# Where the absolute sums of the feed-forward weights are taken: VectorE's reduction, or ScalarE's absolute value with a second result

## The chip, the core and the metric

One core of one Trainium2 chip runs the whole kernel. Its engines have a queue of instructions each and run them in order: TensorE (PE, with its weight loads shown apart as PEld), VectorE (DVE), ScalarE (ACT), GpSimd (POOL), and SyncE (SP), which here issues nearly all transfers. The metric is the device time of one execution in microseconds; what is shown as the time before is the median of three runs. The profile is of one further execution: its span goes from the first to the last instruction, its time is taken around it.

## What is computed

A cross-attention layer and a feed-forward layer with quantized weights, on four batches of 512 tokens by 512 features, float32. Cut to what matters here:

```python
x = x + attention(layernorm(x), ctx, pos, Wq, Wkv, Wout, bout)     # 32 heads of 16, rotary positions
x = x + ffn(layernorm(x), w_fc, w_proj)                            # 512 -> 2048 -> 512

def ternarize_weights(w):
    gamma = jnp.mean(jnp.abs(w))                                   # one number for a whole matrix
    return jnp.sign(jnp.round(w / (gamma + EPS))) * gamma

def bitlinear(x, w):
    xn = layer_norm(x)
    x_hat = absmax_quant(xn)                                       # 128 levels a side
    return jnp.einsum('bsd,od->bso', x_hat, ternarize_weights(w))

def ffn(x, w_fc, w_proj):
    return bitlinear(jax.nn.gelu(bitlinear(x, w_fc), approximate=False), w_proj)
```

Both weight matrices have 2048 x 512 elements. Before their signs can be formed, the sum of all absolute values of the matrix has to be known. That sum is what the change is about.

## The kernel before

**Two parts.** The attention runs first, up to about 565 us; the feed-forward follows. The weights are summed and turned into signs during the attention, between its other work, and the signs go back to DRAM (wfc_d, wproj_d), from where the feed-forward loads them.

**Attention.** There are 32 groups (4 batches, 8 groups of 4 heads), and a group has 8 units. A unit of kind "l" makes scores (lp, L524) of which only the row maxima are wanted: VectorE takes them in one reduction of 128x1024 (mx, L538). A unit of kind "s" makes the scores again, transposed (sp, L563), adds the negated maxima by another matmul (L571, from mrows), and ScalarE takes the exponential (es, L575). Two s units together feed the weighted sum of values (av, L585), eight matmuls. lp runs some 12 units ahead of sp. lp and sp share three PSUM tiles (tag "s"), used in turn, so a new score tile needs the one three before it drained: an lp by VectorE, an sp by ScalarE.

**Order.** The order on all five queues is written out by hand. The units are strung together, s and l in turn, and cut into bursts of three. In burst k the kernel first runs what was put off to its start (run(k): copies out of PSUM by ScalarE, such as L430, L497, L381, L554 and L602), then the burst's units, then what was put off to its end (run(k, 1)), then the weighted sums that are due, then a "chore": projections, transposes, and the like (L344, L374, L550), which have one PSUM tile of their own. put_off(k, f, 1) puts f at the end of burst k.

**The weights.** The two matrices are cut into 32 pieces of 128x512 (chunk). At units 2 and 6 of every group from the first on, sum_chunk loads one piece into a buffer of tag "wch" (four buffers) and puts its sum off to the end of the fourth burst after. Each sum is one column of wsums. At groups 8 and 16 mean_abs adds 16 columns (L694) and sums over the partitions by a matmul. From group 9 on, at the same units and behind sum_chunk, sign_chunk loads a piece again into a "wch" buffer; two bursts later POOL compares it (low, L686), three bursts after that VectorE forms the signs (ws, L684), and one burst later SP stores them (L688).

So in groups 0 to 15 each group has two sums; from group 9 to 24 it has two pieces of signs. SP issues the loads of both (L667, L680), the stores of rotated queries and keys (L424), the loads of the stacks (L510), and the transfers of the attention's result (L603, L614, L615, L619, L623), all in one order; a load into a "wch" buffer waits at the head of SP's queue until that buffer is free.

**ScalarE's tables.** Sin, Exp and Gelu are each announced by one small activation ahead of their use (L817, L1015) or come with the first use (L247); the copies, casts and squares between them are on ScalarE too.

Of the kernel before, what the change touches and what calls it, by code (L numbers as in the profile page):

```python
# [11 lines left out]
AF = mybir.ActivationFunctionType  # L12
ALU = mybir.AluOpType
AX = mybir.AxisListType
# [17 lines left out]
def xattn_ffn(  # L32
# [13 lines left out]
    nc = tc.nc  # L46
# [248 lines left out]
    def put_off(k, f, end=0):  # L295
        later[end].setdefault(k, []).append(f)
# [70 lines left out]
    def tokens(b, t, ready=0):  # L367


        def step(tp, _):  # L370
            if t == 0:
                xT[b] = big.tile([P, KD, S], F32, name=f"xT{b}", tag="w4")
            for k in range(KD):
                nc.tensor.transpose(  # L374
                    tp[:, k * P : (k + 1) * P], xh[b, t][:, k * P : (k + 1) * P], ident
                )

        def post(tp, k):
            put_off(
                k + 1,  # L380
                lambda: nc.scalar.copy(  # L381
                    xT[b][:, :, t * P : (t + 1) * P], tp.rearrange("p (k n) -> p k n", k=KD)
                ),
            )
            if b > 0 and t + XH < NT:
                put_off(k + 1, lambda: normed(b, t + XH), 1)

        return Chore(f"xtp{b}_{t}", 1, step, post, 0.7, ready)
# [95 lines left out]
    def values(b, t):  # L484
        def step(p, k):
            product(
                p,
                ctx_tiles[b][:, k, t * P : (t + 1) * P],
                wkv_sb[:, k, D : 2 * D],
                k == 0,  # L490
                k == KC - 1,
            )

        def post(p, k):
            put_off(
                k + 1,
                lambda: nc.scalar.copy(  # L497
                    va[b % 2][:, t, 0 : NH * VS].rearrange("p (h d) -> p h d", d=VS)[:, :, 0:HD],
                    p.rearrange("p (h d) -> p h d", d=HD),
                ),  # L500
            )

        return Chore(f"vp{b}_{t}", KC, step, post)
# [43 lines left out]
    def place_maxima(i):  # L547
        def step(tp, _):
            for t in range(NT):
                nc.tensor.transpose(tp[:, t * P : (t + 1) * P], mparts[i % 2][:, t, :], ident)  # L550

        def post(tp, k):
            mrows[i] = apool.tile([P, S], F32R, name=f"mrows{i}", tag="mrows")
            put_off(k + 1, lambda: nc.scalar.copy(mrows[i], tp))  # L554

        return Chore(f"mtp{i}", 1, step, post, 0.7)
# [96 lines left out]
    wsums = const.tile([P, 2 * NW], F32, name="wsums")  # L653
# [3 lines left out]
    def chunk(c):  # L657
        if c < NW:
            k, n = divmod(c, FB)
            rows, cols = slice(k * P, (k + 1) * P), slice(n * 512, (n + 1) * 512)  # L660
            return wfcT[rows, cols], wfc_d[rows, cols], gam_fc
        rows = slice((c - NW) * P, (c - NW + 1) * P)
        return wprojT[rows, :], wproj_d[rows, :], gam_pr

    def sum_chunk(c, k):
        w = apool.tile([P, D], F32, name=f"wm{c}", tag="wch", bufs=4)
        nc.sync.dma_start(w, chunk(c)[0])  # L667
        put_off(
            k + 4,
            lambda: nc.vector.tensor_reduce(  # L670
                wsums[:, c : c + 1], w, AX.X, ALU.add, apply_absolute_value=True
            ),
            1,
        )

# [111 lines left out]
    c = heads(0, 0, "k")  # L787
# [4 lines left out]
    for t in range(NT):  # L792
        c = tokens(0, t)
# [5 lines left out]
    c = heads(0, 0, "q")  # L799
# [5 lines left out]
    for what in "kq":  # L805
        c = heads(0, 1, what)
# [14 lines left out]
    c = values(0, 0)  # L821
# [8 lines left out]
    for n in range(FIRST + 1):  # L830
# [11 lines left out]
        if n == NU + 1:  # L842
            c = place_maxima(0)
# [65 lines left out]
    for k, burst in enumerate(bursts):  # L909
        run(k)  # L910
        for kind, s in burst:
# [21 lines left out]
            if u in (2, 6):  # L933
                c = 2 * i + u // 4
                if c < 2 * NW:
                    sum_chunk(c, k)
                c -= 18
                if 0 <= c < 2 * NW:
                    sign_chunk(c, k)
# [21 lines left out]
        while due and due[0][0] <= k:  # L961
            _, j, c, e = due.pop(0)
# [17 lines left out]
        while True:  # L980
            if open_chore is None:
# [5 lines left out]
                elif queue and queue[0].ready <= k and not used_bank and credit >= queue[0].cost:  # L987
                    c = queue[0]
# [286 lines left out]
```

## Time and profile before

| | |
|---|---|
| time before, median of 3 runs | 841.18 us (840.21 to 842.34) |
| time of the profiled execution | 843.25 us |
| its span | 840.9 us |
| mean granted TensorE clock | 0.995 |
| POOL busy | 297.6 us (35%) |
| the sums, L670: VectorE, 128x512 float32 | 32 of 672 ns mean, 21.5 us |
| loads of the pieces for the sums, L667 | 32 of 256 KB, issued 48.6 to 314.7 us |
| forming the signs, L684: VectorE | 32, from 214.4 to 478.4 us |

How to read what follows. A row of a group of instructions gives line, engine, operation, what is written and read by the program's names, shapes and count; then busy time in us and the mean of one in ns; then the idle time of the engine just before them and what ended most of it. A row of the timeline gives start and length in us; rows that follow each other on an engine are merged (x2), and brackets give the idle time before and its releaser. A row of waits gives the total, how many times, and the longest. A row of a stretch gives its bounds and length, then busy time (and instructions) of PE, PEld, DVE, ACT and POOL, the granted TensorE clock, the share of the DMA engines and GB/s. A matmul's row overlaps the next one's, since they are pipelined; the distance from start to start says more than the length.

### The profile page before, as it was taken

Reading aid. Unit: us, or ns where it says so; the run is one execution under the profiler, and the core shown is the slowest. Engines: PE = TensorE matmul, PEld = TensorE weight load, DVE = VectorE, ACT = ScalarE, POOL = GpSimd, SP = SyncE. Lnnn points to the kernel's source line nnn. Section 1 sums busy time; section 2 is a strip of 40 time slices with the busy share of each in tenths; the row PEclk is TensorE's granted clock in tenths of the full one; section 3 lists DMA queues with packets and bytes.
Section 4 is the critical chain, followed back from the end, with each engine's and each line's share of the span. In section 5 each row is a group of like instructions: output and inputs, shape, how many; then the busy total and the mean of one; then the engine's idle time right before and its main releaser. Section 6 shows DMA issues by size and latency. Waiting matters only on the chain.

```text
span 840.9 us, 14326 instructions
## 1 busy us (share of the span) xinstructions
PE 816.2 (97%) x5572; PEld 435.0 (52%) x5572; DVE 613.9 (73%) x858; ACT 456.9 (54%) x604; POOL 297.6 (35%) x299
## 2 busy tenths in 40 slices
PE   8999999999999999999999999999999999999996
PEld 5234433444333334333333334337678888888885
DVE  7799778797878888787777867825465864964755
ACT  3256666575665546656555655576234544554442
POOL 2546274555823637576425621301000100100000
PEclk9999999999999999999999999999999999999999
DMA  7768595687585578949446657532000100100101
GB/s 247 215 209 300 188 329 186 204 292 258 197 296 164 171 265 258 314 168 301 159 151 215 225 179 277 182 110 88 1 0 1 51 1 0 51 1 1 51 0 51
DMA packets 75923, 133.65 MB, mean 159 GB/s; under 512 B 12240, under 2 KB 13776, under 8 KB 75344
## 3 DMA queue, kind: packets, MB, share of 16 engines
q1 hardware_dynamic: 74928, 132.08, 46.4%
q8 instruction: 44, 0.72, 0.3%
q10 hardware_dynamic: 928, 0.66, 0.3%
q14 instruction: 23, 0.19, 0.1%
HBM read 77.73 MB, written 53.94 MB: 157 GB/s over the span
## 4 chain that ended last, share of the span: by engine, by line
PE 81%; DVE 12%; issue 3%; POOL 1%; DMA 1%; ACT 1%; ACTq 0%; DVEq 0%; POOLq 0%; SPq 0%
PE hp L1048 14%; PE fp L1086 14%; PE av L585 12%; PE sp L563 8%; PE lp L524 7%; DVE mx L538 6%; PE sp L571 5%; PE qpq L344 5%; PE op L344 4%; PE vp L344 3%; PE kpk L344 3%; PE op L1167 2%; PE mtp L550 1%; PE xtp L374 1%; PE tot L1106 1%
## 5 line engine op out<-in xcount | busy, mean ns | idle before, releaser
L538 DVE TENSOR_REDUCE mx<-lp 128x2 f32<-128x1024 f32 x256 | 305.1, 1215 | 88.2 <-PE lp L524 87.9
L575 ACT ACTIVATE es<-sp 128x1024 f32<-128x1024 f32 x256 | 254.6, 1024 | 148.9 <-PE sp L571 140.7
L585 PE MATMUL av<-es,va 128*32 128x512 f32 x1024 | 136.9, 608 | 0.0
L563 PE MATMUL sp<-q_st,k_st 64*128 64x512 f32 x512 | 115.0, 445 | 7.3 <-DVE mx L538 6.2
L524 PE MATMUL lp<-k_st,q_st 64*128 64x512 f32 x512 | 111.8, 434 | 3.8 <-DMA q_st<-sl_q 1.9
L1056 ACT ACTIVATE h<-hp,gam_fc 128x512 f32<-128x512 f32 x64 | 44.1, 689 | 125.6 <-PE hp L1048 125.6
L1086 PE MATMUL fp<-wproj,hh 128*128 128x512 f32 x256 | 102.2, 399 | 0.0
L571 PE MATMUL sp<-mrows,sel 64*128 64x512 f32 x512 | 101.7, 393 | 0.2 <-ACT mrows L554 0.2
L1048 PE MATMUL hp<-dTh,wfc 128*128 128x512 f32 x256 | 100.0, 391 | 1.2 <-ACT dTh L758 1.2
L1048 PE MATMUL hp<-dTl,wfc 128*128 128x512 f32 x256 | 99.8, 390 | 0.2 <-DVE dTl L759 0.2
L1086 PE MATMUL fp<-wproj,hl 128*128 128x512 f32 x256 | 99.7, 390 | 0.0
L1075 DVE TENSOR_TENSOR acc<-acc,h 128x512 f32<-128x512 f32 x56 | 38.6, 690 | 71.4 <-ACT h L1056 71.4
L563 PEld LDWEIGHTS sp<-q_st,k_st 64*128 64x128 f32 x512 | 48.0, 184 | 81.9 <-DVE mx L538 42.3
L524 PEld LDWEIGHTS lp<-k_st,q_st 64*128 64x128 f32 x512 | 48.2, 185 | 75.1 <-ACT es L575 38.7
L624 POOL TENSOR_TENSOR aT<-aT,rb 128x512 f32<-128x512 f32 x16 | 22.0, 1374 | 129.7 <-DMA rb<-rden_d 108.3
L344 PE MATMUL qpq<-xT,wq_sb 128*32 128x512 f32 x512 | 63.5, 599 | 0.7 <-ACT xT L381 0.7
L1048 PEld LDWEIGHTS hp<-dTh,wfc 128*128 128x128 f32 x256 | 48.1, 188 | 12.0 <-ACT dTh L758 2.1
L1086 PEld LDWEIGHTS fp<-wproj,hh 128*128 128x128 f32 x256 | 48.1, 188 | 10.4 <-issue 0.7
L1048 PEld LDWEIGHTS hp<-dTl,wfc 128*128 128x128 f32 x256 | 48.1, 188 | 10.4 <-DVE dTl L759 0.5
L1086 PEld LDWEIGHTS fp<-wproj,hl 128*128 128x128 f32 x256 | 48.1, 188 | 10.3 <-issue 0.7
L571 PEld LDWEIGHTS sp<-mrows,sel 64*128 64x128 f32 x512 | 48.3, 185 | 5.9 <-ACT mrows L554 0.8
L224 POOL TENSOR_SCALAR r_a<-mv 128x1 f32<-128x1 f32 x16 | 4.7, 294 | 127.8 <-DVE mv L734 127.8
(149 smaller groups left out, 1054.9 us busy)
## 6 DMA issues: line engine op xcount, KB each, us to landing
k_st<-k_d SPq DMA_DIRECT2D x31, 512.0 KB
q_st<-q_d SPq DMA_DIRECT2D x31, 512.0 KB
av_d<-avs SPq DMA_DIRECT2D x32, 256.0 KB
k_d<-sh_k SPq DMA_DIRECT2D x30, 256.0 KB
k_d<-sl_k SPq DMA_DIRECT2D x30, 256.0 KB
q_d<-sh_q SPq DMA_DIRECT2D x30, 256.0 KB
q_d<-sl_q SPq DMA_DIRECT2D x30, 256.0 KB
wm<-in_wfcT SPq DMA_DIRECT2D x16, 256.0 KB
```

The lines of the kernel that those rows point to most:

```text
L344: nc.tensor.matmul(p[j * HP : (j + 1) * HP, :], w[:, j * HP : (j + 1) * HP], x, start=start, stop=stop,)
L524: nc.tensor.matmul(lp[:, h, :], q_st[i][rows, r, t * P : (t + 1) * P], k_st[i][rows, r, :], start=True, stop=True,)
L538: nc.vector.tensor_reduce(mx[i][:, t, :, r], lp, AX.X, ALU.max, negate=True)
L563: nc.tensor.matmul(sp[:, h, :], k_st[i][rows, r, c * P : (c + 1) * P], q_st[i][rows, r, :], start=True, stop=False,)
L571: nc.tensor.matmul(sp[:, h, :], sel[rows, r, :], mrows[i][rows, :], start=False, stop=True)
L575: nc.scalar.activation(es, sp, AF.Exp, scale=1.0 / math.sqrt(HD))
L585: nc.tensor.matmul(av[j * HP : (j + 1) * HP, :], va[b % 2][:, c, v0 : v0 + HP], es[r][:, h, :], start=c == 0, stop=c == NT - 1,)
L624: nc.gpsimd.tensor_tensor(aT[b][:, n, :], aT[b][:, n, :], rb, ALU.mult)
L1048: nc.tensor.matmul(hp, wfc_sb[k][:, f * P : (f + 1) * P], dT[b][half][:, k, :], start=half == 0 and k == 0, stop=half == 1 and k == KD - 1,)
L1056: nc.scalar.activation(hid[b, f], hp, AF.Gelu, scale=gam_fc[:, 0:1])
L1075: nc.vector.tensor_tensor(acc[b][0], old, x, ALU.add)
L1086: nc.tensor.matmul(outs[b][t], parts[b, f][half][:, t * P : (t + 1) * P], wproj_sb[f], start=half == 0 and f == 0, stop=half == 1 and f == ...
```

## The change

The sum of a piece moves from VectorE to ScalarE. There it is an activation with the function Abs, which writes the absolute values back over the piece and gives, as a second result (accum_out), their sum along the row. It is put off to the same burst, and stands at the end of that burst in ScalarE's order instead of VectorE's. The loads, the buffers, mean_abs and sign_chunk stay as they are; sign_chunk loads its piece again, so nothing reads the values written over.

```diff
@@ -667,9 +667,7 @@
         nc.sync.dma_start(w, chunk(c)[0])
         put_off(
             k + 4,
-            lambda: nc.vector.tensor_reduce(
-                wsums[:, c : c + 1], w, AX.X, ALU.add, apply_absolute_value=True
-            ),
+            lambda: nc.scalar.activation(w, w, AF.Abs, accum_out=wsums[:, c : c + 1]),
             1,
         )
```

## The prediction

> **What bounds the kernel now.** I read the page's busy times first, then the chain, then the costliest groups, the waits of TensorE's weight loads while the sums run, and last the timeline at each of the 32 sums.
>
> ```profile
> PE 816.2 (97%) x5572; PEld 435.0 (52%) x5572; DVE 613.9 (73%) x858; ACT 456.9 (54%) x604; POOL 297.6 (35%) x299
> ...
> PE 81%; DVE 12%; issue 3%; POOL 1%; DMA 1%; ACT 1%; ACTq 0%; DVEq 0%; POOLq 0%; SPq 0%
> ...
> L538 DVE TENSOR_REDUCE mx<-lp 128x2 f32<-128x1024 f32 x256 | 305.1, 1215 | 88.2 <-PE lp L524 87.9
> L575 ACT ACTIVATE es<-sp 128x1024 f32<-128x1024 f32 x256 | 254.6, 1024 | 148.9 <-PE sp L571 140.7
> ```
>
> TensorE holds 81% of the chain, VectorE 12%. So VectorE matters only where TensorE waits for a maximum (L538): the three tiles of tag "s" are shared by scores for the maxima (lp) and for the exponentials (sp), and each new tile waits until the one three before it is drained, by VectorE (lp) or ScalarE (sp).
>
> ```profile
> L670 DVE TENSOR_REDUCE wsums<-wm x32: 622/676/680, 63.5 to 323.6; 128x1 f32<-128x512 f32 x32
> ...
> 60.00:330.00 270.00, 266.26 (x2068) 106.28 (x2060) 225.50 (x285) 163.36 (x194) 146.62 (x123) 0.99 0.70 236
> ...
> PEld sp L563 <- DVE mx L538: 20.9, 37, 1.9
> PEld lp L524 <- ACT es L575: 19.8, 36, 0.8
> ```
>
> The sums run from 63.5 to 323.6 us. In 60 to 330 VectorE is busy 225.5 of 270 us (84%), ScalarE 163.4 (61%), so the move goes from the fuller engine to the emptier. But the weight loads' waits of some 20 us for either engine overstate it: most lie under a matmul that still runs. I therefore took TensorE's starts in the timeline. After a pair of matmuls into one tile the next pair usually starts 0.23 to 0.33 us later; only what is beyond is a stall. In front of sp (L563) that excess sums to about 9.7 us over 60 to 330, and most of it is not behind a sum.
>
> **What is removed.** 32 reductions of 0.672 us (21.5 us of VectorE); the next instruction behind one starts 0.55 to 0.60 us after it. At 16 of the 32 VectorE then sits idle 0.08 to 1.36 us until TensorE delivers the next lp: nothing gained there. Behind the others I looked whether the maximum that comes next is one TensorE stalls for, and took the lesser of the stall and the time that the maximum can move. The largest:
>
> ```profile
> 271.65 0.66 PE L550 MATMUL mtp<-ident,mparts 128*128 128x128 f32 x4
> ...
> 272.18 0.63 DVE L670 TENSOR_REDUCE wsums<-wm 128x1 f32<-128x512 f32 x1
> ...
> 272.72 2.34 DVE L538 TENSOR_REDUCE mx<-lp 128x2 f32<-128x1024 f32 x2
> ...
> 273.98 0.50 PE L563 MATMUL sp<-q_st,k_st 64*128 64x512 f32 x2 [1.67 <-DVE mx L538]
> ```
>
> The maxima start 0.54 us after the sum does, so 0.54 of the 1.74 us go; the rest is there because five other VectorE instructions came before. In the same way: 0.42 at 75 us (stalls of 0.09 and 0.33, maxima 0.60 earlier), 0.24 at 105.9, 0.55 at 173.6 to 174.8 (stalls 0.52 and 0.33, maxima 0.55 earlier), 0.19 at 205.6, 0.33 at 302.2, 0.54 at 310.1 to 311.2 (0.22 for the addition L646, 0.32 for sp). Sum: 0.42+0.24+0.55+0.19+0.54+0.33+0.54 = 2.8 us.
>
> **The clock.** The stall at 273.98 has a second price:
>
> ```profile
> 265.24:268.65 3.41, 2.88 (x30) 1.16 (x26) 3.41 (x5) 1.94 (x2) 1.53 (x2) 1.00 0.76 202
> ...
> 272.07:275.48 3.41, 1.57 (x13) 0.78 (x11) 3.41 (x5) 1.25 (x2) 0.00 (x0) 1.00 0.40 132
> 275.48:278.90 3.42, 3.42 (x20) 0.59 (x16) 2.75 (x6) 1.39 (x2) 0.00 (x0) 0.50 0.27 85
> ```
>
> TensorE was busy 1.57 of 3.41 us, and the next 3.41 us were granted half the clock: 1.7 us of work lost. With 0.54 us less stall that stretch would be busy 2.11 of 3.41 us, 62%, between this 46% and the 84% (2.88) that brought no dip. I count the dip as gone in the profiled execution. The three timed runs lie between 840.21 and 842.34 us, a spread wider than the dip, so some may not have had it; against their median I count half, 0.85 us.
>
> [...]
>
> **What is added.** Each sum becomes an ACTIVATE (Abs, written back over w) plus whatever delivers the second result. No row shows either. Nearest for the pass: Square, 128x512 float32 from SBUF to SBUF. For the delivery: nothing below, another full pass above; nearest is the smallest ACTIVATE, one column.
>
> ```profile
> L1073 ACT ACTIVATE sq<-h 128x512 f32<-128x512 f32 x60 | 37.7, 628 | 0.0
> ...
> L817 ACT ACT_TABLE_LOAD x1 | 1.3, 1283 | 0.0
> ...
> L817 ACT ACTIVATE exp<-ones 128x1 f32<-128x1 f32 x1 | 0.2, 203 | 0.0
> ```
>
> So A, the time for one sum, is 0.63 to 1.26 us; I take 0.63+0.20 = 0.83 (26.6 us in all). The Abs is queued in run(k, 1), behind the last exponential of burst k. Behind it wait the copies of burst k+1 (L602, L430, L381, L497, L554) and the next exponentials, and for those TensorE's tile three later and the weighted sums (L585). I listed for all 32 places the ScalarE idle time that follows (0 to 2.6 us), passed the remaining delay on, and set it against the time from the end of each delayed instruction to the start of the matmul that needs it. Copies have 0.6 us or more, av 1.8 us or more, and exponentials 0.38 or more, but for two places, this one and its twin at 181:
>
> ```profile
> 78.99 0.59 ACT L602 COPY avs<-av 128x512 f32<-128x512 f32 x1 [0.17 <-PE av L585]
> 79.55 0.59 ACT L381 COPY xT<-xtp 128x512 f32<-128x512 f32 x1
> 80.28 1.94 ACT L575 ACTIVATE es<-sp 128x1024 f32<-128x1024 f32 x2
> ...
> 81.38 0.50 PE L524 MATMUL lp<-k_st,q_st 64*128 64x512 f32 x2
> ```
>
> The first exponential ends at 81.31 and lp starts 0.08 us later, 0.055 being the least anywhere. The Abs stands before 78.99; of its 0.83 us the gaps 0.17 and 0.14 take 0.31, 0.52 reach the exponential, 0.49 TensorE. Twice that is 1.0 us of loss. The same working gives 0.6 us at A = 0.63, 1.6 at 1.0, 3.1 at 1.2, 3.7 at 1.26, 5.3 at 1.43: one more place at a time loses its slack.
>
> **What moves with it.** No DMA is added. The SP queue waits for these sums to free a "wch" buffer:
>
> ```profile
> SPq L680 <- DVE wsums L670: 35.9, 12, 7.4
> ```
>
> That is from SP's own waits (total, times, longest). Queued behind it are stores and loads of the next stacks. Comparing the ends at sums 17 to 31: the Abs would end 0.3 to 0.8 us later at six of them, up to 3.6 us earlier (272.80 against 269.3) at the rest; no stall of TensorE in that stretch ends with a DMA, so I count nothing. The total over the sums (L694, 188.62) now waits for ScalarE: the last Abs of that layer ends near 187.6, 1 us ahead; without that cover the signs start later, which feed only DRAM.
>
> **Sum.** In the profiled execution (span 840.9, time 843.25, the highest of the four times shown): -2.8 + 1.0 - 1.7 = -3.5, a span of 837.4. Against the median: 841.18 - 2.8 + 1.0 - 0.85 = 838.5 us. Below 0.3% (2.5 us) a measurement of this kernel can't tell a change from none.
>
> **Rivals.**
> 1. The gain goes into other VectorE work. L331 took 1.52 us at 170 beside a POOL instruction, against 0.54 elsewhere; casts L542 1.18 against 0.17. If the later three gains (0.54, 0.33, 0.54) are spent in such collisions and the dip stays, 1.4 - 1.0 remain: 840.8. For it: five other instructions in front of 273.98. Against: where maxima follow the sum directly, nothing is between.
> 2. The wait changes sides: exponentials held behind the Abs. It needs a dear second result, at L602, L381, L430 and the exponentials of sums 2, 7, 12, 14, 16, 18 and 20. It beats the 2.8 us from A = 1.16 and is slower by 2.5 from A = 1.43: 841.2 - 2.8 + 5.3 = 843.7. For it: no row shows the read. Against: one-column work costs 0.20.
> 3. Abs needs a table load of its own and Exp another after it: two of 1.283 for each sum, A = 3.2, loss 50.5: 889. Against: three loads in all, though Copy, casts and Square run between Exp and Gelu. [...]
> 4. The pass itself takes ScalarE a multiple of VectorE's time. [...] Against: 0.628 for Square on the same shape and type. [...]
> 5. All 9.7 us of stalls before sp go, and the dip: 841.2 - 9.7 - 1.7 + 1.0 = 830.8. Against: only 2.8 stand behind sums.
>
> **How the numbers follow.** Forecast 58%, its own range 836 to 840.5; 46 of it faster by over 2.5 us, 12 within. Rival 1 14% (within). Rival 2 18% (16 slower, 2 within). Rival 3 3%. Rival 4 1%. Rival 5 6%. So faster 0.52, same 0.28, slower 0.20. The range goes from 834.5, part of the way to rival 5, to 843.7, rival 2.
>
> **What would show it.** L670 as ACTIVATE near 0.63 us and a short second row on ACT; three table loads; VectorE's busy time down 21.5 us, ScalarE's up 20 to 27; the stalls at 75, 173 and 274 gone or near 1.2; new ones of half a microsecond where xT is copied (81 and 181); clock 1.00 near 275. Wrong if the ACT rows for a sum exceed 1.2 us, or TensorE waits for es at more than those two places.

## The result, and the profile after

| | before | after |
|---|---|---|
| median on the same chip, 20 runs each | 841.68 us (839.76 to 845.64) | 839.46 us (836.41 to 841.86) |
| profiled execution: time, span | 843.25, 840.9 us | 839.09, 837.3 us |
| mean granted clock of the profiled execution | 0.995 | 0.999 |

The ratio of the times is 0.9971, with an interval of 0.9959 to 0.9983: some 2.4 us faster (1.4 to 3.5). The predicted time was 838.5 us, the predicted span of the profiled execution 837.4.

Lines of the changed kernel's page: the span, busy time by engine, shares of the chain, and the two groups that drain the score tiles.

```profile
span 837.3 us, 14374 instructions
...
PE 812.9 (97%) x5572; PEld 434.6 (52%) x5572; DVE 597.8 (71%) x826; ACT 474.1 (57%) x668; POOL 297.2 (35%) x299
...
PE 81%; DVE 12%; DMA 2%; issue 2%; ACT 1%; POOL 1%; ACTq 0%; SPq 0%; DVEq 0%; POOLq 0%
...
L538 DVE TENSOR_REDUCE mx<-lp 128x2 f32<-128x1024 f32 x256 | 305.2, 1216 | 100.0 <-PE lp L524 99.7
L575 ACT ACTIVATE es<-sp 128x1024 f32<-128x1024 f32 x256 | 254.9, 1025 | 139.3 <-PE sp L571 130.7
```

The shape of the chain is what it was. VectorE has 32 instructions and 16 us less, ScalarE 64 instructions and 17 us more; the forecast had 21.5 less and 20 to 27 more. The rows of the sums are that long (21.5, and 20.1 + 6.4), but rows that overlap count once in the busy time, and on VectorE forming the signs of the first matrix rose from 14.6 to 17.5 us. VectorE's idle time ahead of the maxima rose from 88.2 to 100.0 us, so most of the time it won went into waiting for TensorE.

Groups of instructions on ScalarE in the changed kernel: the new line and the table loads.

```profile
L670 ACT ACTIVATE wm<-wm 128x512 f32<-128x512 f32 x32 | 20.1, 628 | 0.0
L670 ACT ACTIVATION_READ_ACCUMULATOR wm<-wm 128x1 f32 x32 | 6.4, 199 | 0.0
...
L247 ACT ACT_TABLE_LOAD x1 | 1.3, 1283 | 3.9 <-issue 3.9
L815 ACT ACT_TABLE_LOAD x1 | 1.3, 1283 | 0.0
L1013 ACT ACT_TABLE_LOAD x1 | 1.3, 1283 | 0.0
```

Each sum is two instructions: the pass, 0.628 us, as long as Square was, and a read of the accumulated sum, 0.199 us. There are three table loads, as before.

Three stretches of the changed kernel, with busy time by engine, granted clock, and DMA: first 60 to 330 us, then two beats of 3.41 us around the stall that stood at 274 us (now at 271). In the trace of the kernel before, half clock begins at 29.72, at 275.48 and, behind TensorE's last work, at 838.68 us; the first two stretches last 3.41 us each, and the second and third begin 72 and 237 such beats behind the first. I divided each trace into beats of this length, counted from a half clock of its own. From the start of the span they lie elsewhere from one execution to another (the first half clock begins at 29.72 us there, at 29.25 in the sixth run, at 28.8 in the tenth); those of this one are counted back from 835.45 us, where half clock begins behind TensorE's last work.

```profile
60.00:330.00 270.00, 265.60 (x2072) 106.75 (x2070) 212.78 (x257) 182.25 (x261) 149.33 (x126) 1.00 0.72 241
268.84:272.25 3.41, 2.17 (x20) 1.01 (x12) 3.38 (x6) 1.39 (x3) 0.00 (x0) 1.00 0.36 126
272.25:275.66 3.41, 3.22 (x24) 1.09 (x26) 3.38 (x7) 1.65 (x2) 0.25 (x1) 1.00 0.63 202
```

VectorE went from 225.5 to 212.8 us in the first, ScalarE from 163.4 to 182.3. TensorE is busy 2.17 of the 3.41 us of the beat with the stall (1.57 before), and no half clock follows.

The timeline of the changed kernel at that stall, TensorE and VectorE:

```profile
269.28 0.66 PE L550 MATMUL mtp<-ident,mparts 128*128 128x128 f32 x4
...
269.57 0.32 DVE L618 RECIPROCAL den<-den 128x32 f32<-128x32 f32 x1
269.80 2.29 DVE L538 TENSOR_REDUCE mx<-lp 128x2 f32<-128x1024 f32 x2
...
271.02 0.50 PE L563 MATMUL sp<-q_st,k_st 64*128 64x512 f32 x2 [1.08 <-DVE mx L538]
```

From the last transposition group to sp it is 1.74 us, where 0.59 is usual: a stall of 1.15. Before, the same distance was 2.33, a stall of 1.74. The sum that stood between the reciprocal and the maxima is gone, and so are 0.59 us.

SP's own wait for a "wch" buffer in the changed kernel (total, times, longest); the numbers of lines behind the change are two less:

```profile
SPq L678 <- ACT wm L670: 32.5, 9, 5.7
```

Before it was 35.9 us in 12 waits, the longest 7.4. No stall of TensorE hangs on it in either kernel.

**Where the 3.6 us between the two profiled spans lie.** I compared the start of the first sp of each of the 32 groups in the two traces. The changed kernel is 1.78 us ahead at group 0 already, before any sum is formed: the other execution had half a clock at 29.7 us, this one had none. It wins 1.85 us between groups 13 and 14 (0.59 of stall and about 1.25 of half clock). At the other steps 2.7 us are won and 2.7 lost, and from group 19 on the lead stays at 3.6. So apart from the two half clocks this pair differs by 0.6 us, and the first of the two cannot come from the change.

The steps with sums 1, 5, 13 and 28 and 29 are won about as forecast: 0.54, 0.25, 0.59 and 0.63 us, where the prediction had 0.42, 0.24, 0.55 and 0.87. The largest loss is 1.24 us from group 16 to 17. POOL and VectorE there, first in the changed kernel:

```profile
318.88 1.28 POOL L416 TENSOR_TENSOR oth_k<-oth_k,trig 128x512 f32<-128x512 f32 x1
320.11 1.30 POOL L417 TENSOR_TENSOR rot_k<-rot_k,trig 128x512 f32<-128x512 f32 x1
...
318.89 1.31 DVE L542 CAST mparts<-mx 128x16 fp32r<-128x16 f32 x1
320.23 1.21 DVE L543 TENSOR_TENSOR mparts<-mx,mparts 128x16 fp32r<-128x16 f32 x1
```

and the same two VectorE instructions before:

```profile
323.31 0.18 DVE L542 CAST mparts<-mx 128x16 fp32r<-128x16 f32 x1
323.52 0.18 DVE L543 TENSOR_TENSOR mparts<-mx,mparts 128x16 fp32r<-128x16 f32 x1
```

With the sums gone, the two instructions fall on POOL's rotation of the keys; before, they had ended when it began (at 324.04 us). The traces of the first and the tenth run lose 1.19 us at the same step.

For the experiments I therefore use, beside the ratio, the **full-clock span**: span times mean granted clock of each run, averaged over the runs. TensorE being busy 97% of the span, that is by my estimate about what the run would have lasted at full clock throughout. (It also counts the half clock behind TensorE's last work, 1.9 to 5.1 us at the end of the kept spans, when TensorE has no work left; this adds spread, so only averages are compared.) Over 61 runs of the kernel before it is 837.22 us, over 31 of the changed kernel 834.62: a gain of 2.6 us. The mean granted clock is 0.9966 and 0.9964 (two standard errors are 0.0004 and 0.0006), so the change has no gain in clock. The two profiled executions are not typical: at full clock both come to 836.4 us, 0.9 below the average of the kernel before and 1.8 above that of the changed one. Values behind ± below are two standard errors.

### The profile page after: what moved, and what is told of

Same layout as the page of the kernel before. It is cut to its first block, busy times and chain, and to the rows that moved or that the text cites. A ratio compares the mean times of both kernels' runs of the same rounds, so it can differ in the third digit from the quotient of the medians.

```text
span 837.3 us, 14374 instructions
## 1 busy us (share of the span) xinstructions
PE 812.9 (97%) x5572; PEld 434.6 (52%) x5572; DVE 597.8 (71%) x826; ACT 474.1 (57%) x668; POOL 297.2 (35%) x299
## 4 chain that ended last, share of the span: by engine, by line
PE 81%; DVE 12%; DMA 2%; issue 2%; ACT 1%; POOL 1%; ACTq 0%; SPq 0%; DVEq 0%; POOLq 0%
PE hp L1046 14%; PE fp L1084 14%; PE av L585 12%; PE sp L563 8%; PE lp L524 7%; DVE mx L538 7%; PE sp L571 5%; PE op L344 4%; PE qpq L344 4%; PE kpk L344 3%; PE vp L344 3%; PE op L1165 2%; PE mtp L550 1%; DVE ws L682 1%; PE warm L344 1%
```

## The experiments

**1. No sums at all.** The loads stay, the sums are left out on both engines, and wsums is filled with constants. This takes away what the change takes from VectorE and adds nothing to ScalarE.

```diff
+    nc.gpsimd.memset(wsums[:, 0:NW], 18.05)
+    nc.gpsimd.memset(wsums[:, NW : 2 * NW], 9.03)
...
-        put_off(
-            k + 4,
-            lambda: nc.scalar.activation(w, w, AF.Abs, accum_out=wsums[:, c : c + 1]),
-            1,
-        )
```

> Leaves out the 32 sums on both engines (the columns of wsums are set to constants instead). Theory (VectorE's sums hold up maxima that TensorE stalls for, 2.8 us; ScalarE's sums give back 1.0 us): 2.8 us and about half a clock dip (0.85) less than before, ratio 0.9956, and some 1.0 us less than the changed kernel; in the profile the stalls before sp behind a sum are gone and none is new where xT is copied. Rival (the gain of the changed kernel is only where half-clock windows fell): at equal granted clock no difference to before, ratio 0.998 to 1.002.

Measured: 838.76 us against 842.36 of the kernel before on that chip, ratio 0.9965 (0.9950 to 0.9979); full-clock span 834.63 ± 0.25, from 837.38 ± 0.44. What VectorE is relieved of is worth 2.75 us. The changed kernel's full-clock span, 834.62, is the same: the sums on ScalarE cost nothing that can be measured, within some 0.5 us, where the expectation had 1.0 us between the two kernels.

**2. Only the eight sums that stand before a stall.** The seven sums of the prediction's list and sum 7 (at 119 us) go to ScalarE; the other 24 stay on VectorE.

```diff
-            lambda: nc.scalar.activation(w, w, AF.Abs, accum_out=wsums[:, c : c + 1]),
+            lambda: (
+                nc.scalar.activation(w, w, AF.Abs, accum_out=wsums[:, c : c + 1])
+                if c in (1, 5, 7, 13, 17, 25, 28, 29)
+                else nc.vector.tensor_reduce(
+                    wsums[:, c : c + 1], w, AX.X, ALU.add, apply_absolute_value=True
+                )
+            ),
```

> Only the sums 1, 5, 7, 13, 17, 25, 28 and 29, those behind which a stall of TensorE stood, move to ScalarE; the other 24 stay on VectorE. Theory: the whole 2.8 us and the half dip are won and nothing is given back, ratio to before 0.9956, some 1.0 us under the changed kernel. Rival (the relief of VectorE counts in proportion to its busy time): a quarter of what the changed kernel won, 0.6 us, ratio 0.9993.

Measured: 838.55 us, ratio 0.9959 (0.9944 to 0.9975); full-clock span 834.66 ± 0.37. Eight sums moved bring what 32 bring, so moving the other 24 wins nothing that can be measured. The further 1.0 us that was expected from leaving them did not come.

**3 and 4. Two passes on ScalarE; two sums on VectorE.** In the third, each sum has a further Abs ahead of the accumulating one. In the fourth, all is on VectorE as before, but every sum is taken twice.

```diff
 # third
+                nc.scalar.activation(w, w, AF.Abs),
                 nc.scalar.activation(w, w, AF.Abs, accum_out=wsums[:, c : c + 1]),
 # fourth
+            lambda: [
+                nc.vector.tensor_reduce(
+                    wsums[:, c : c + 1], w, AX.X, ALU.add, apply_absolute_value=True
+                )
+                for _ in range(2)
+            ],
```

> As the changed kernel, with a second absolute value over each piece on ScalarE, so that one sum takes 628 + 628 + 199 = 1455 ns there. Theory (delay beyond the slack of each place is lost): loss 5.5 us instead of 1.0, so 4.5 us above the changed kernel, ratio to before about 1.002. Rival (ScalarE, 57% busy, hides it all): like the changed kernel, 0.997. Second rival (each us in ScalarE's order is lost one to one): 32 x 0.628 = 20 us above the changed kernel, 1.021.

> As before, with each sum taken twice on VectorE (0.6 us more at each of the 32 places). Theory (the same slack working, applied to the maxima behind each place): 7.7 us above before, ratio 1.009. Rival (VectorE at 84% has room, only clock windows decide): within 1 us of before. Second rival (one to one): 19 us above before, 1.023.

Two passes on ScalarE: 841.43 us, ratio 0.9987 (0.9975 to 0.9998); full-clock span 836.78 ± 0.59, 2.2 above the changed kernel, half of the 4.5 expected. Two sums on VectorE: 852.2 us, ratio 1.0115 (1.0096 to 1.0133); full-clock span 846.29, 8.9 above the kernel before, where 7.7 was expected. So some 0.7 us more for each sum (0.66 on ScalarE and 0.71 on VectorE, from start to start) costs four times as much on VectorE as on ScalarE, and the first pass on ScalarE is free where the second is not. TensorE's own waits from 60 to 345 us, with two sums on VectorE:

```profile
PE sp L563 <- DVE mx L538: 9.0, 19, 1.2
PE lp L524 <- DVE mx L538: 1.7, 1, 1.7
PE mtp L550 <- DVE x_sb L646: 0.9, 1, 0.9
```

The wait for the maxima is 9.0 us in 19 places; in the kernel before it is 3.4 in 8. The same view with two passes on ScalarE shows the other side:

```profile
PE sp L563 <- DVE mx L538: 4.1, 11, 1.1
PE lp L524 <- ACT es L575: 0.5, 2, 0.3
...
PE xtp L374 <- ACT xT L381: 0.4, 2, 0.2
```

TensorE now waits for exponentials and xT: 0.18 and 0.27 us at each of the two places that the prediction had named for a single pass, 0.9 of the 2.2 us. Waits for the maxima are longer too in this execution, 4.1 us against 3.3 in the changed kernel. The place at 79 us in this kernel, ScalarE and TensorE:

```profile
75.74 1.03 ACT L575 ACTIVATE es<-sp 128x1024 f32<-128x1024 f32 x1 [0.66 <-PE sp L571]
...
78.88 1.95 ACT L575 ACTIVATE es<-sp 128x1024 f32<-128x1024 f32 x2
...
79.05 0.66 PE L374 MATMUL xtp<-ident,xh 128*128 128x128 f32 x4 [0.18 <-ACT xT L381]
79.97 0.50 PE L524 MATMUL lp<-k_st,q_st 64*128 64x512 f32 x2 [0.27 <-ACT es L575]
```

and the same place in the changed kernel:

```profile
75.48 1.02 ACT L575 ACTIVATE es<-sp 128x1024 f32<-128x1024 f32 x1 [0.65 <-PE sp L571]
76.40 0.62 ACT L670 ACTIVATE wm<-wm 128x512 f32<-128x512 f32 x1
76.92 0.19 ACT L670 ACTIVATION_READ_ACCUMULATOR wm<-wm 128x1 f32 x1
77.02 0.58 ACT L602 COPY avs<-av 128x512 f32<-128x512 f32 x1
77.48 0.60 ACT L381 COPY xT<-xtp 128x512 f32<-128x512 f32 x1
77.96 1.97 ACT L575 ACTIVATE es<-sp 128x1024 f32<-128x1024 f32 x2
...
78.48 0.66 PE L374 MATMUL xtp<-ident,xh 128*128 128x128 f32 x4
79.07 0.50 PE L524 MATMUL lp<-k_st,q_st 64*128 64x512 f32 x2
```

From the exponential at 75.48 to the one at 77.96 it is 2.48 us. Before, with no Abs between, it was also 2.48 (77.80 to 80.28). With two passes it is 3.14. Three things made room for the one pass. The rows overlap: from the start of Abs to the start of the copy behind it is 0.62 us, not 0.628 + 0.199. The copy L602 had waited 0.27 us start to start. And the instructions behind it had stood farther apart (0.56 and 0.73 us from start to start) than they do behind the Abs (0.46 and 0.48). 0.27 + 0.10 + 0.25 = 0.62.

**5 and 6. The one sum before the half clock, and the seven others.** As in the second, with c in (25,), and with c in (1, 5, 7, 13, 17, 28, 29). These were meant to tell the clock term from the stalls.

```diff
+                if c in (25,)                          # fifth
+                if c in (1, 5, 7, 13, 17, 28, 29)      # sixth
```

> Only sum 25, the one in front of the longest stall (at 274 us), moves to ScalarE. Theory (the stall makes the half-clock stretch behind it): the stall falls from 1.74 to some 1.2 us and the half-clock stretch near 275 is gone; the step from group 13 to group 14 is 1.85 us shorter in the profile and the other groups after the start are unchanged; median some 1.0 to 1.4 us less than before, ratio 0.9983 to 0.9988. Rival (half-clock stretches fall at random): 0.5 us less, 0.9994, and a stretch at half clock near 275.

> The sums 1, 5, 7, 13, 17, 28 and 29 move to ScalarE; 25 and the rest stay on VectorE. Theory: 2.3 us less than before, all of it in the groups with these sums; the step from group 13 to group 14 is not shorter through a smaller stall (1.7 us again at 271 to 274). Ratio 0.9973. Rival (what counts is the half-clock stretch at 275 alone): within 0.5 us of before at equal granted clock.

The one sum: 840.81 us, against 841.55 before, 0.7 less where 1.0 to 1.4 were expected; ratio 0.9995 (0.9984 to 1.0006), which tells it from no change neither way; full-clock span 836.05 ± 0.81 against 837.04 ± 0.38. Its profile has the stall at 1.15 us and no half clock behind it, and its step from group 13 to 14 is 1.84 us shorter, as forecast. But by group 10 it has lost 1.6 us, where its program is still that of the kernel before, so the total can't be read from one execution. Inconclusive as to time; the mean granted clock is 0.9962, against 0.9967, no gain.

The seven others: 840.31 us, ratio 0.9984 (0.9969 to 0.9999); full-clock span 835.10 ± 0.63, a gain of 1.9 where 2.3 was worked out. Its trace holds the surprise. TensorE at the stall that was left in, then three beats of this execution (counted from its half clock at 29.25 us):

```profile
272.75 0.50 PE L563 MATMUL sp<-q_st,k_st 64*128 64x512 f32 x2 [1.68 <-DVE mx L538]
```

```profile
268.19:271.60 3.41, 2.88 (x24) 1.25 (x20) 3.34 (x7) 2.11 (x3) 1.75 (x2) 1.00 0.23 70
271.60:275.01 3.41, 2.10 (x17) 0.96 (x20) 3.41 (x5) 1.42 (x3) 0.00 (x0) 1.00 0.48 157
275.01:278.43 3.42, 3.22 (x28) 1.08 (x24) 3.39 (x6) 1.21 (x2) 0.00 (x0) 1.00 0.35 114
```

The stall has its full length, but begins in one beat and ends in the next: neither falls below 2.10 of 3.41 us, and the clock stays at 1.00. In the kernel before's profile it lay in one beat, busy 1.57, and half a clock followed. The step from group 13 to 14 is 1.24 us shorter than there, which is what that half clock cost. So whether this stall brings the half clock depends on where it falls, and that differs from execution to execution.

**7 and 8. No rotary arithmetic on POOL, before and after.** POOL's three products and sums (L416 to L418) are left out and the subtraction L420 is a fill with zeros, in the kernel before (7) and in the changed one (8). This asks what collisions with POOL do to VectorE's stalls, and to the change.

```diff
-                e.tensor_tensor(oth, oth, trig[:, b % 2, 1, :], ALU.mult)
-                e.tensor_tensor(rot, rot, trig[:, b % 2, 0, :], ALU.mult)
-                e.tensor_tensor(rot, rot, oth, ALU.add)
                 e.tensor_copy(high, rot)
-                e.tensor_tensor(low, rot, high.bitcast(F32), ALU.subtract)
+                e.memset(low, 0.0)
```

> The kernel before with POOL's rotation of queries and keys left out (three of its five instructions for each; of the other two the copy stays and the subtraction becomes a fill with zeros). It is the ground for e8. Theory (VectorE's casts and sign instructions are stretched when POOL reads at the same time): L542 falls from 463 ns mean to under 300, L684 from 917 to under 820, and the kernel is 2 to 6 us faster than before. Rival (the stretch comes from something else): these means stay.

> The changed kernel with the same part of POOL's work left out as in e7. Theory (part of what VectorE's relief brings is given back where its instructions now meet POOL's, at 219 and 319 us in the changed kernel): without POOL's reads no new stalls at sp near 222 and 326. Between e7 and e8 the difference is then only the stalls that still stand behind sums in e7, 1.0 to 2.8 us. Rival (what is given back is ScalarE's own cost): stalls of half a microsecond appear in front of lp or xtp, behind es or xT.

Kernel before without it: 834.77 us, ratio 0.9918 (0.9901 to 0.9935). Changed kernel without it: 833.65 us, ratio 0.9907 (0.9890 to 0.9924). Full-clock spans 829.63 ± 0.95 and 828.79 ± 1.11. Taking the arithmetic from POOL gains three times what the change gains, 7.4 us at full clock where 2 to 6 were expected, and with it gone the change brings some 0.8 us (± 1.5) instead of 2.6. The means of L542 and L684 fall as expected, from 463 to 273 and from 917 to 803 ns. POOL's queue is also shorter by three instructions each time; how much of the 7.4 us is collisions and how much is that, no run tells. In the kernel before, most of the stalls of the prediction's list are gone without the rotary arithmetic: at 173, 205, 105 and 302 us there is none, only that at 272 keeps its 1.74. So at these four places the sum alone did not make TensorE wait; it needed the rotary work on POOL as well. A collision, in the changed kernel, VectorE and POOL:

```profile
219.03 1.30 POOL L420 TENSOR_TENSOR sl_k<-rot_k,sh_k 128x512 f32<-128x512 f32 x1
...
219.13 1.75 DVE L682 SCALAR_TENSOR_TENSOR ws<-ws,gam_fc,low 128x512 f32<-128x512 f32 x1
...
221.44 3.48 DVE L538 TENSOR_REDUCE mx<-lp 128x2 f32<-128x1024 f32 x3
...
222.70 0.50 PE L563 MATMUL sp<-q_st,k_st 64*128 64x512 f32 x2 [0.40 <-DVE mx L538]
```

Forming the signs took 1.75 us beside POOL's subtraction, against 0.74 elsewhere, and TensorE waited for the maximum behind it. TensorE's waits from 60 to 345 us in the changed kernel:

```profile
PE sp L563 <- DVE mx L538: 3.3, 10, 1.1
PE gp L697 <- DVE total L692: 0.7, 1, 0.7
PE kpk L344 <- DVE x_sb L646: 0.5, 1, 0.5
```

By this view it waits for the maxima 3.3 us in 10 places, against 3.4 in 8 before: old places are shorter, and new ones have come (222.7, 283.8, and one at 326 for the total, L692). Without the rotary arithmetic the changed kernel has neither that at 222 nor that at 326. The kernel without any sums has both (223.6 and 326.4 us), so they are not ScalarE's doing. The one at 326 stands behind the two stretched instructions at 319 us shown above.

**9. Three passes on ScalarE**, to see whether row lengths or distances from start to start predict the loss.

```diff
+                nc.scalar.activation(w, w, AF.Abs),
+                nc.scalar.activation(w, w, AF.Abs),
                 nc.scalar.activation(w, w, AF.Abs, accum_out=wsums[:, c : c + 1]),
```

> As the changed kernel, with three absolute values over each piece on ScalarE instead of one. Theory, mended after e3 (what counts is the distance from start to start in ScalarE's queue, 0.54 us for a further pass and 0.62 for the pass with its read, not the lengths of the rows): 1.70 us for a sum, loss about 9 us by the slack of the 32 places, 9 us above the changed kernel, ratio to before 1.007. Rival (by the rows' lengths, 3 x 0.628 + 0.199 = 2.08 us): loss 16 us, 15 above the changed kernel, 1.016. Second rival (ScalarE hides it): like e3, 0.999.

Measured: 847.67 us, ratio 1.0074 (1.0059 to 1.0090); full-clock span 843.39 ± 0.57, 8.8 above the changed kernel. The expectation from start to start had about 9, that from row lengths 15. But the 0.54 us that it gave a further pass is the distance from a pass to its read. From one pass to the next it is 0.66 us here, so one sum takes 1.95 us, not 1.70, and the hit does not tell the two measures apart. TensorE's waits from 60 to 345 us:

```profile
PE av L585 <- ACT avs L602: 3.1, 4, 0.8
PE sp L563 <- DVE mx L538: 2.2, 5, 1.3
PE xtp L374 <- ACT xT L381: 1.7, 2, 0.8
PE mtp L550 <- ACT rot_q L430: 1.0, 2, 0.6
PE kpk L344 <- ACT xT L381: 0.8, 1, 0.8
```

Now the copies behind the sums are what TensorE waits for most. The waits for VectorE have shrunk (3.3 in the changed kernel), perhaps because TensorE comes later to them; no run shows that.

**10. The changed kernel once more**, on the chip of the ninth.

> The changed kernel once more, on the same chip as e9, to see its mean granted clock and its span at equal clock beside those of before. Theory: ratio 0.997 again, mean granted clock as before's (0.9963 to 0.9967), so that span times granted clock shows the gain, 2.6 us. Rival (the change also saves half-clock stretches): a mean clock higher by 0.001 or more, which is 0.85 us.

Measured: 838.99 us against 841.86, ratio 0.9969 (0.9958 to 0.9980); mean granted clock 0.9966 against 0.9967; full-clock span 834.71 ± 0.54 against 837.25 ± 0.56. The gain repeats, and again without any gain in clock.

## Why the prediction came out right, point by point

**The maxima that come earlier, -2.8 us: right in size.** Without sums the gain at full clock is 2.75 us (first run), and the seven sums of the list with one more bring all of it (second run). The stall at 274 was worked out to 1.2 us and is 1.15. Place by place it is shown in part: the steps with sums 1, 5, 13, 25, 28 and 29 are won in the traces, but 1.2 us are lost again from group 16 to 17. How the average still comes to 2.6, the few traces do not show.

**ScalarE's cost, +1.0 us: the mechanism right, the size wrong.** The step that failed is A = 0.63 + 0.20 = 0.83: ScalarE's rows were added by their lengths, while VectorE's sums had been counted from start to start. From start to start A is 0.62. The gaps, too, were read from the idle time in brackets (0.17 + 0.14), and start to start they are 0.62 at the first of the two places. So nothing is lost there; measured is 0.0 ± 0.5 in all. That a loss comes when A grows, at those two places among the first, was shown by the third run. The working's sizes are too large there as well: from start to start a sum takes 1.29 us in the third run and 1.95 in the ninth. The prediction had 3.7 us at 1.26 against 0.6 at 0.63, about 3 more, and the expectation of the ninth run 9 us at 1.70 and 16 at 2.08; 2.2 and 8.8 us above the changed kernel were measured.

**The clock, -0.85 us: not seen.** The half clock behind 274 is gone in the profile, as forecast, and its beat is busy 2.17 us (2.11 forecast). The link is borne out: of the four kept traces with sum 25 on VectorE, three have half a clock behind the stall (before, fourth and seventh run, each with a beat busy 1.57 us), and of the eight without it none. But over all runs the mean granted clock did not rise. Two sizes were too large. The half clock cost 1.25 us, not 1.7 (sixth run). And half of the executions was too many: moved along the trace of the kernel before, a beat of 3.41 us holds 1.66 us of TensorE's work or less (the most that half clock followed in the kept traces) at only 0.75 of the 3.41 us of positions around the stall. If all positions were equally likely, a fifth of the executions would have the half clock, worth some 0.3 us (an estimate from these two numbers), which the mean clock is too coarse to show. The other half clock, near 29 us, comes and goes in both kernels (29.7 before, 28.8 in the tenth run).

The two errors, +1.0 and -0.85, nearly cancel, which is luck: the sum forecast -2.65 us, and 2.6 was measured at full clock. For the profiled execution it is luck altogether: 837.4 was forecast and 837.3 came, but of the 3.6 us 1.78 lie before the first sum, 1.25 are the half clock, 0.59 are the one stall, and all else comes to nothing, where -1.8 had been worked out for stalls and ScalarE together.

**The rivals.** The first, the gain going into collisions of VectorE with POOL, is there and took part of the gain: 1.2 us from group 16 to 17, the step after sums 28 and 29, in the traces of the changed kernel (twice) and of no sums, and new waits at 222.7 and 326 us, both gone without the rotary arithmetic. On the average it did not take the whole. The second, exponentials held behind Abs, does not hold for the changed kernel; it is at work in the ninth run, while in the third, at 1.29 us for a sum, the kernel is still not slower than before (full-clock span 836.78 against 837.38), where this rival had it so from 1.16 on. The third fell with three table loads (Abs ran between the exponentials without one of its own), the fourth with 0.628 us for the pass. The fifth wanted all of the 9.7 us; no sums at all gave 2.75.

**SP's waits** fell from 35.9 to 32.5 us and cost nothing, as forecast. The wait for the total (L692) is new, 0.7 us, but is there without any sums on ScalarE too, so the cover of the last Abs was enough.

**What stays open.** The steps between groups differ between executions of one program, by up to 0.25 us at a step in the two traces of the changed kernel and by 1.6 us over ten groups between the kernel before and the fifth run. That this is VectorE's instructions meeting POOL's is not shown; I have no run that fixes it. That 2.6 shrinks to about 0.8 us without the rotary arithmetic has an interval too wide to put a size on it. No kernel tried beats the changed one clearly: no sums (0.9965) and eight sums on ScalarE (0.9959) lie within its interval.

## What to carry to other kernels

Relieving a busy engine is worth only the instructions that stand before a wait of the bounding engine: find those in the timeline, take the lesser of stall and advance, and leave the rest out. Count both engines in the same measure, from start to start, and set what is added against the gaps from start to start at each place; here a pass of 0.63 us was free where a second cost 2.2 us. Do not book a clock dip seen in one profile as a gain: find the beats of that execution, ask at how many of their positions the dip would come, and compare spans at equal granted clock over many runs.

## What the runs showed of the hardware

The read of the accumulated sum has a row of 0.199 us but holds ScalarE's queue for less: it starts 0.52 us after the Abs, and at 19 of the 32 places the next instruction starts 0.09 us after it. Where one Abs over a piece follows another over the same piece, they start 0.66 us apart (third and ninth run). Two VectorE instructions that ran beside a POOL TENSOR_TENSOR of 1.3 us in the changed kernel took more than twice the time they take elsewhere: forming the signs 1.75 us at 219 against 0.74 at 272, the cast of the maxima 1.31 at 319 against 0.18 in the kernel before. In the kernel before without POOL's rotary arithmetic the mean of that cast fell from 463 to 273 ns.

In the twelve kept traces, each divided into its own beats of 3.41 us from 6 to 820 us, half clock began eleven times, each time behind a beat in which TensorE was busy 1.49 to 1.66 us. Two beats of 1.65 and 1.66 us (near 565 us in the sixth and the fifth run) brought none, and no beat of 1.73 us or more did. So a stall of one length brought half a clock where it lay in one beat (busy 1.57 us), and none where it lay across two (busy 2.88 and 2.10).
